# Opening of a four-block recurrent kernel: x as first transfer, fills of spare rows moved, first batch's q and k split by halves on two engines ahead of the channel mix

## The chip, the cores and the metric

The kernel runs on one core of a Trainium2 chip. The metric is the device time of one execution in microseconds, lower is better. The core's engines each run their own stream of instructions in order and wait for each other through semaphores: PE (matmul, with weight loads shown as PEld), DVE (vector), ACT (activation functions), POOL (GpSimd), and SP, which issues all the transfers of this kernel.

## The reference

A stream x of shape (4, 1024, 128) passes through four blocks. Each block normalizes x, computes an attention-like branch s and a feed-forward branch g from the normalized values, and adds s times silu(g) to x:

```python
x = L0_attn_query
xn = _layernorm(x, axis=-1)
s = _L0_attn_ref(xn, L0_attn_in_proj_w, L0_attn_out_proj_w)
g = _silu(_L0_ffn_ref(xn, L0_ffn_W_r, L0_ffn_W_k, L0_ffn_W_v, L0_ffn_mu_r, L0_ffn_mu_k))
x = x + s * g
...
```

The change touches block 0 alone. Its s is attention with 16 heads of 8 dimensions, rotary embedding of q and k, and a window of 250 positions:

```python
q, k = _apply_rope(q, k)
delta = pos[:, None] - pos[None, :]
mask = (delta >= 0) & (delta < CONTEXT)
scores = jnp.einsum('bhtd,bhsd->bhts', q, k) * D ** (-0.5)
scores = jnp.where(mask[None, None, :, :], scores, jnp.finfo(scores.dtype).min)
attn = jax.nn.softmax(scores, axis=-1)
x = jnp.einsum('bhts,bhsd->bhtd', attn, v)
```

Its g is a channel mix, which mixes each position with the one before it and passes it through three matrices:

```python
xr = mu_r * x + (1.0 - mu_r) * x_prev
xk = mu_k * x + (1.0 - mu_k) * x_prev
r = jax.nn.sigmoid(jnp.einsum('btc,dc->btd', xr, W_r))
k = jnp.einsum('btc,dc->btd', xk, W_k)
out = r * jnp.einsum('btc,dc->btd', jnp.square(jax.nn.relu(k)), W_v)
```

Block 1 has causal attention and a mixture of 8 experts, block 2 a full-attention transformer layer and a switch layer, block 3 a state-space layer and two layers of local attention.

## The kernel before

**Layout.** A batch is 1024 positions of 128 channels. Transferred to the chip it is a tile of 128 partitions by 8 by 128; after the norm (`_norm_steps`, two halves of 512 positions each, the power for the reciprocal root on POOL as `ln_rs`) PE turns it (`tr_ps`) and ACT copies it into `xT`, channels by positions.

**Projection and split.** `project(b)` in `_attention` makes q and k of one batch in halves of 512 positions: two matmuls into `proj_ps`, and three DVE operations that apply the rotation (`qd` or `kd`, and `rope_t`). To multiply with bf16 inputs at nearly fp32 precision, `_split` writes a value as three bf16 parts: a cast, a subtraction, a cast and a subtraction, lines 196 to 199. In the kernel before all four run on POOL, once for the 1024 positions of q and once for those of k. The parts are stored to DRAM (`qx`, `kx`, line 282) and read back by `load(n)` in another arrangement (lines 318 and 321): three copies into `q9` and nine into `k9` for each unit. A unit is four heads of one batch, so block 0 has 16 units; three pairs of `q9` and `k9` take turns.

**Spare rows.** `q9` and `k9` have 128 rows. Rows 0 to 71 hold the 3 by 3 products of parts. Rows 72 to 74 of `q9` later take the three parts of minus the row maximum (`negr`, line 404), which meet ones in `k9`. The remaining rows of `q9` must be zero. At the start rows 64 to 127 of all three `q9` are filled with 0.0 on DVE and those of all three `k9` with 1.0 on POOL (line 854), and 3 rows of zeros are stored to DRAM for the units from the fourth on. Two tiles `va` for the values are filled with 1.0 on POOL (line 859).

**Maxima.** `maxima(n)` multiplies q and k of a unit (`max_ps`) in 14 steps and DVE reduces each to the row maximum (`neg`). `attend(n)` does the multiplication again (`sc`), with the maximum taken off by the extra rows, then the exponential on ACT (`pt`) and the product with the values (`o_ps`).

**Channel mix.** `_channel_mix` makes half a batch in four steps: `dx` (POOL, line 658) and `xrk` (DVE), the key `kp` with a ReLU on ACT and a square on POOL (line 668), the receptance `rv` with a sigmoid, and the value.

**Order.** Matmuls, transposes and POOL's `_tt` calls keep the program's order; a scheduler places the rest on each engine by its own estimate when the program is built, so the order in the source is only part of the order that runs. `_blocks012` writes the opening: the norm of batch 0 runs, then two streams are interleaved in proportion, `begin` (projection of batch 0, loads of units 0 and 1, 14 steps of maxima of unit 0, the split of the maxima, 5 steps of maxima of unit 1) and `other` (norms of batches 1 to 3 and eight half-batch mixes), with the silu steps at the end of `other`. Then `rest` runs the units: maxima of the next unit beside the weights of this one, and on three of four units parts of the next batch's projection. All transfers are issued by SP in its own order; the first ones are w0, w1, r1, rope, and then x of batches 0 and 1.

Of the kernel before, what the change touches and what calls it, by code (L numbers as in the profile page):

```python
# [29 lines left out]
P = 128  # L30
# [157 lines left out]
def _run(steps):  # L188
    for step in steps:
        if step:  # L190
            step()
# [27 lines left out]
def _attention(k, pool, mode, xT, w, out, rope=None):  # L219
# [19 lines left out]
    def project(b):  # L239

        xb = xT[:, b, 1 : T + 1]
        steps = []
        va = dense["va", b] = k.va[b % 2]

        def half(what, hf):
            cols = slice(512 * hf, 512 * hf + 512)

            def step():
                if hf == 0:
                    dense[what] = pool.tile([P, T], F32, tag="d", name=f"{what}d", bufs=2 if mode == "window" else 1)  # L250
                d = dense[what] if hf == 0 else dense.pop(what)
                ps = ps2("proj_ps")
                matmul(ps[:, 0, :], lhsT=w[what], rhs=xb[:, cols], start=True, stop=True)
                if rope is not None:
                    matmul(ps[:, 1, :], lhsT=w[what + "s"], rhs=xb[:, cols], start=True, stop=True)
                bias = w.get("b" + what, 0.0)
                if mode == "window":

                    t2 = pool.tile([P, 512], F32, tag="rope_t", name="rope_t", bufs=2)
                    nc.vector.tensor_tensor(d[:, cols], ps[:, 0, :], rope[:, 0, cols], ALU.mult)  # L260
                    nc.vector.tensor_tensor(t2, ps[:, 1, :], rope[:, 1, cols], ALU.mult)
                    nc.vector.tensor_tensor(d[:, cols], d[:, cols], t2, ALU.add)
                else:
                    nc.scalar.activation(d[:, cols], ps[:, 0, :], AF.Identity, bias=bias)
                if rope is not None and mode != "window":
                    t2 = pool.tile([P, 512], F32, tag="rope_t", name="rope_t", bufs=2)
                    nc.scalar.activation(t2, ps[:, 1, :], AF.Identity, bias=w.get("b" + what + "s", 0.0))
                    nc.gpsimd.tensor_tensor(d[:, cols], d[:, cols], rope[:, 0, cols], ALU.mult)
                    nc.gpsimd.tensor_tensor(t2, t2, rope[:, 1, cols], ALU.mult)
                    nc.gpsimd.tensor_tensor(d[:, cols], d[:, cols], t2, ALU.add)  # L270
                if hf == 1:
                    parts = pool.tile([P, 3, T], BF16, tag="parts", name=f"{what}p", bufs=1)
                    _split(nc, nc.gpsimd, d, parts, d)
                    dense[what, "parts"] = parts

            return step

        def store(what):
            def step():

                flat = k.tc.dram_tile([3, P, T], BF16, name=f"{what}x")
                nc.sync.dma_start(flat.rearrange("s p t -> p s t"), dense.pop((what, "parts")))
                dense[what, b] = flat.rearrange("s (d h) t -> (s d) h t", h=H)

            return step

        def values(i):
            def step():
                ps = ps1("v_ps")
                for c in range(4):  # L290
                    t0 = P * (4 * i + c)
                    matmul(
                        ps[:, c * P : c * P + P], lhsT=xb[:, t0 : t0 + P], rhs=w["v"], start=True, stop=True
                    )
                vh = va[:, 4 * i : 4 * i + 4, 0 : H * (HD + 1)].rearrange("p c (h d) -> p c h d", d=HD + 1)
                of = ps.rearrange("p (c h d) -> p c h d", c=4, d=HD)
                if "bv" in w:
                    bv = w["bv"].rearrange("p (h d) -> p h d", d=HD)
                    for c in range(4):
                        nc.vector.tensor_tensor(vh[:, c, :, 0:HD], of[:, c], bv, ALU.add)  # L300
                else:
                    nc.scalar.copy(vh[:, :, :, 0:HD], of)

            return step

        for what in ("q", "k"):
            steps += [half(what, 0), half(what, 1)]

        return steps + [store("q"), lambda: None, store("k"), values(0), values(1)]
# [527 lines left out]
def _blocks012(k, t):  # L837
# [7 lines left out]
    with ExitStack() as ctx:  # L845
        pool_of = lambda name, side="left": k.tc.tile_pool(name=name, bufs=1, side=side)
        k.ps = ctx.enter_context(k.tc.tile_pool(name="ps", bufs=2, space=PSUM))
        with pool_of("w1") as wp:


            k.q9, k.k9 = ([wp.tile([P, 4, T], BF16, name=f"{n}9_{i}") for i in range(3)] for n in "qk")
            for q9, k9 in zip(k.q9, k.k9):
                nc.vector.memset(q9[64:P], 0.0)
                nc.gpsimd.memset(k9[64:P], 1.0)
            k.zeros = k.tc.dram_tile([3, 4 * T], BF16, name="zeros")
            nc.sync.dma_start(k.zeros, k.q9[2][72:75].rearrange("p h t -> p (h t)"))
            k.va = [wp.tile([P, NT, H * (HD + 1) + 32 - HD - 1], F32, name=f"va_{i}") for i in range(2)]
            for t_ in k.va:
                nc.gpsimd.memset(t_, 1.0)
            early = ctx.enter_context(ExitStack())  # L860
            wp0 = early.enter_context(pool_of("w0", "right"))
            w0 = wp0.tile([P, 9 * P + 2], F32, name="w0")
            nc.sync.dma_start(w0, t["w0"])
            names = ("q", "qs", "k", "ks", "v", "o", "wr", "wk", "wv")
            w = {n: w0[:, i * P : i * P + P] for i, n in enumerate(names)}
            mu_r, mu_k = w0[:, 9 * P : 9 * P + 1], w0[:, 9 * P + 1 : 9 * P + 2]

            w1 = wp.tile([P, 4 * P + 10], F32, name="w1")
            nc.sync.dma_start(w1, t["w1"])
            r1 = wp.tile([P, 2 * P + E8], F32, name="r1")  # L870
            nc.sync.dma_start(r1, t["r1"].to_broadcast([P, 2 * P + E8]))
            gates = {}

            def to_block1(b, gp, pool):

                g = xn[:, tiles_of(b), :]
                lg = {}

                def logits():
                    lg[0] = pool.tile([P, NT, E8], F32, name="lg", bufs=2)  # L880
                    of = lambda i: xT[:, b, 1 + i * P : 1 + i * P + P]
                    _logits(k, lg[0], of, w1[:, 4 * P + 2 : 4 * P + 10], r1[:, 2 * P : 2 * P + E8])

                def gate():
                    gates[b] = _gating(k, pool, gp, lg[0], b)

                return _update_steps(k, b, xin[b]) + _fm_steps(k, g, xT, b) + [logits, None, gate]

            with pool_of("a0") as pool:
                rope = pool.tile([P, 2, T], F32, name="rope")  # L890
                nc.sync.dma_start(rope, t["rope"][:, 0])
                wa = {n: w[n] for n in names[:6]}
                held = {}
                normed = [
                    [lambda b=b: held.update({b: _x_tile(k, xin[b])})]
                    + _norm_steps(k, lambda b=b: held[b], xn[:, tiles_of(b), :])
                    + _fm_steps(k, xn[:, tiles_of(b), :], xT, b)
                    for b in range(B)
                ]
                normed[0].insert(1, normed[1].pop(0))  # L900
                begin, rest = _attention(k, pool, "window", xT, wa, s, rope)
                _run(normed[0])
                mix = [_channel_mix(k, pool, w, mu_r, mu_k, n) for n in range(2 * B)]
                other = []
                for b in range(B):
                    other += (normed[b + 1] if b + 1 < B else []) + mix[2 * b] + mix[2 * b + 1]
                _interleave(other + _silu_steps(k, range(B)), begin)
                plan = {}
                for b in range(B - 1):
                    _put(plan, to_block1(b, wp, wp), _behind(b))  # L910
                rest(plan)
                last = to_block1(B - 1, wp, wp)
            early.close()

            with pool_of("w2", "right") as wp2:
                NW = 14 * P
                w2 = wp2.tile([P, NW + 20], F32, name="w2")
                nc.sync.dma_start(w2, t["w2"])
                r2 = wp2.tile([P, 3 * P + E8], F32, name="r2")
                nc.sync.dma_start(r2, t["r2"].to_broadcast([P, 3 * P + E8]))  # L920
                lg2 = wp2.tile([P, NTILE, E8], F32, name="lg2")
                _blocks12(k, t, wp, pool_of, gates, last, (w1, r1, w2, r2, lg2))
# [1268 lines left out]
```

## Time and profile before

| | |
|---|---|
| median of 3 runs | 3529.68 us (3518.91 to 3532.71) |
| the profiled execution | 3530.33 us, its span 3528.6 us |
| PE busy | 3137.5 us (89%) |
| DVE busy | 2458.7 us (70%) |
| ACT busy | 1985.6 us (56%) |
| POOL busy | 1415.6 us (40%) |
| mean DMA rate | 42 GB/s over the span |
| first statistics on x (DVE) | starts at 12.31 us |
| first operation of the rotation, `qd` (DVE) | starts at 24.64 us |
| store of q's parts, of k's parts issued (SP) | 37.46 us, 53.44 us |
| first `max_ps` matmul, first `sc` matmul (PE) | 67.46 us, 108.21 us |

Times in the trace count from the span's start. A row of the trace in order of time gives start, length, engine, line, operation, output and input, how many of a kind were merged, and in brackets how long the engine had been idle and what ended that. Where many rows of one kind are merged, the length is that of the whole group. DVE's calls in block 0 go through a helper and all show line 60, PE's matmuls show line 104 or 108, so the tiles' names tell them apart. Line numbers of the changed kernel are six higher behind the first edit.

### The profile page before, as it was taken

What the parts mean: (1) busy time and instruction counts of PE and PEld (TensorE: products, weight loads), DVE (VectorE), ACT (ScalarE), POOL (GpSimd) and SP (SyncE); (2) the same over time, 40 slices, a digit from 0 to 9 for tenths busy, and PEclk for the clock granted to TensorE, in tenths of its full rate; (3) what the DMA queues carried; (4) which work ended last, traced back from release to release, by engine and by line L of the source; (5) the groups of instructions that cost most, each with busy time, mean ns of one, the idle gap of its engine ahead of it and who ended that gap; (6) DMA issues with size and microseconds to landing.
All of it is one profiled execution on the core that took longest, in us unless ns stands there. A gap on an engine that the chain in (4) does not pass through costs nothing.

```text
span 3528.6 us, 63440 instructions
## 1 busy us (share of the span) xinstructions
PE 3137.5 (89%) x23982; PEld 1693.8 (48%) x24121; DVE 2458.7 (70%) x4929; ACT 1985.6 (56%) x4191; POOL 1415.6 (40%) x1969
## 2 busy tenths in 40 slices
PE   4898988999989988889998989986899989989997
PEld 3444445664434434422333323322666767766665
DVE  7667663447777865788785686844788778777675
ACT  2444453346555554455666766664665656666664
POOL 5555553003323251120340321014766656755653
PEclk8999999999999999999999999998899999999999
DMA  3322312201222211011111211102110011011010
GB/s 101 71 63 55 73 42 87 59 28 47 52 50 60 42 51 31 21 45 28 39 45 45 66 35 26 30 7 73 29 37 16 20 25 24 18 24 28 21 27 21
DMA packets 134085, 146.61 MB, mean 42 GB/s; under 512 B 80642, under 2 KB 108298, under 8 KB 126474
## 3 DMA queue, kind: packets, MB, share of 16 engines
q1 hardware_dynamic: 131732, 138.34, 16.3%
q0 software_dynamic: 2048, 4.20, 0.4%
q8 instruction: 191, 3.13, 0.4%
q14 instruction: 114, 0.93, 0.1%
HBM read 94.42 MB, written 30.11 MB: 35 GB/s over the span
## 4 chain that ended last, share of the span: by engine, by line
PE 58%; DVE 19%; ACT 9%; POOL 8%; issue 4%; DMA 2%; SPq 0%; ACTq 0%; POOLq 0%; DVEq 0%
PE o_ps L104 11%; PE max_ps L104 10%; PE sc L104 10%; DVE neg L60 6%; ACT pt L451 4%; PE op L104 4%; PE hp L104 3%; POOL rn L1573 2%; PE proj_ps L104 2%; PE lsc L1481 1%; PE lo_ps L1481 1%; PE ag_ps L1481 1%; PE qk_ps L1481 1%; PE wo_ps L1481 1%; DVE xn L60 1%
## 5 line engine op out<-in xcount | busy, mean ns | idle before, releaser
L451 ACT ACTIVATE pt<-sc 128x512 f32<-128x512 f32 (+3 forms) x2432 | 1076.2, 512 | 754.1 <-PE sc L104 698.1
L60 DVE TENSOR_REDUCE neg<-max_ps 128x1 f32<-128x1024 f32 (+6 forms) x1088 | 1171.9, 1101 | 443.6 <-PE max_ps L104 404.8
L104 PE MATMUL sc<-q,k 128*128 128x512 bf16 (+3 forms) x2399 | 643.1, 340 | 94.6 <-ACT pt L451 69.0
L104 PE MATMUL max_ps<-k,q 128*128 128x512 bf16 (+3 forms) x2200 | 611.2, 347 | 73.8 <-DVE neg L60 50.7
L104 PE MATMUL o_ps<-pt,va 128*32 128x512 f32 (+3 forms) x4864 | 562.6, 526 | 16.8 <-POOL pt L421 9.1
L421 POOL TENSOR_SCALAR_AFFINE_SELECT pt<-pt 128x256 f32<-128x256 f32 (+2 forms) x768 | 291.3, 397 | 541.7 <-ACT pt L451 537.0
L104 PEld LDWEIGHTS <-k 128*128 128x128 bf16 x2432 | 185.6, 98 | 531.5 <-issue 415.9
L104 PEld LDWEIGHTS <-q 128*128 128x128 bf16 x2304 | 217.1, 99 | 357.6 <-issue 245.6
L1643 ACT ACTIVATE pr<-lsc,nb,r 128x128 f32<-128x128 f32 x512 | 201.2, 476 | 67.9 <-DVE nb L1635 67.7
L1564 POOL TENSOR_TENSOR qn<-qn,rot 128x512 f32<-128x512 f32 x128 | 166.1, 1303 | 157.8 <-DVE rot L1556 133.2
L1573 POOL TENSOR_TENSOR rn<-ss,neghalf 128x16 f32<-128x16 f32 x64 | 188.5, 2945 | 60.5 <-DVE ss L1571 48.3
L104 PEld LDWEIGHTS o_ps<-pt,va 128*32 128x32 f32 x4864 | 100.1, 109 | 227.1 <-issue 170.8
L196 POOL CAST negp<-neg 128x32 bf16<-128x32 f32 x48 | 10.1, 211 | 477.2 <-DVE neg L60 477.1
L91 POOL TENSOR_TENSOR ln_rs<-ln_ve,neghalf 128x4 f32<-128x4 f32 x72 | 73.8, 1026 | 262.0 <-DVE ln_ve L60 246.5
L728 ACT ACTIVATE h<-hp,eb 128x512 f32<-128x512 f32 x128 | 80.8, 683 | 163.2 <-PE hp L104 157.2
L1481 PE MATMUL qk_ps<-wqkv,hT 128*128 128x512 f32 x256 | 139.2, 628 | 23.7 <-DMA wqkv<-in_w_dram 7.3
L104 PE MATMUL hp<-xT,ew 128*128 128x512 f32 x256 | 127.9, 624 | 15.5 <-DVE neg L60 12.5
L60 DVE SCALAR_TENSOR_TENSOR xn<-op,gates,xn 128x128 f32<-128x128 f32 x256 | 72.0, 344 | 99.2 <-PE op L104 99.2
L104 PEld LDWEIGHTS op<-ew,h 128*128 128x128 f32 x1024 | 124.3, 194 | 19.6 <-issue 16.3
L104 PE MATMUL max_ps<-mask_window,ident 128*128 128x268 bf16 (+1 forms) x432 | 127.0, 294 | 0.0
L104 PE MATMUL op<-ew,h 128*128 128x128 f32 x1024 | 126.2, 277 | 0.1
L104 PEld LDWEIGHTS <-ident 128*128 128x128 bf16 x864 | 85.2, 99 | 65.5 <-issue 24.6
(368 smaller groups left out, 5483.9 us busy)
## 6 DMA issues: line engine op xcount, KB each, us to landing
q<-qx SPq DMA_DIRECT2D x144, 192.0 KB
k<-kx SPq DMA_DIRECT2D x432, 64.0 KB
va<-vb SPq DMA_DIRECT2D x120, 128.0 KB
qx<-qp SPq DMA_DIRECT2D x12, 768.0 KB
kx<-kp SPq DMA_DIRECT2D x12, 768.0 KB
ew<-in_e1w_dram SPq DMA_DIRECT2D x64, 128.0 KB
x<-x SPq DMA_DIRECT2D x16, 512.0 KB
x<-in_x_dram SPq DMA_DIRECT2D x8, 512.0 KB
```

What stands on the lines that cost most here:

```text
L60: r = op(*args, **kw)
L91: nc.gpsimd.tensor_tensor(rs, ve, k.neghalf[:, :n], ALU.pow)
L104: k.tc.keep_in_program_order(k.nc.tensor.matmul(*args, **kw))
L196: eng.tensor_copy(dst[:, 0], src)
L421: nc.gpsimd.affine_select(out=pt, in_=pt, pattern=[[0, 2], [step, pt.shape[2]]], compare_op=ALU.is_ge, fill=0.0, base=base, channel_multip ...
L451: nc.scalar.activation(pt[:, j % 2, :width], sc[:, :width], AF.Exp, scale=scale)
L728: nc.scalar.activation(h[:, hh, :], hp[:, hh, :], AF.Gelu, bias=eb1[:, e, hh : hh + 1])
L1481: pin(nc.tensor.matmul(*args, **kw))
L1564: nc.gpsimd.tensor_tensor(qn[:, i], qn[:, i], rot, ALU.add)
L1573: nc.gpsimd.tensor_tensor(rn, ss.rearrange("p w h -> p (w h)"), k.neghalf[:, : 2 * NH], ALU.pow)
L1643: nc.scalar.activation(t.pr[:, h, :], t.sc[r][:, c, :], AF.Exp, bias=t.nb[r][:, c : c + 1], scale=t.r8[:, h : h + 1])
```

## The change

Four things are done, all in block 0's opening.

- x of batch 0 is the first transfer on SP. Then come w0, rope, x of batch 1, w1 and r1.
- The fills are written at other places. `va_0` is filled on DVE ahead of the first norm, `va_1` on DVE; `spare(i)` fills the spare rows of one pair: pair 0 after the first norm, pairs 1 and 2 behind the first 11 steps of `begin`, that is behind the loads of units 0 and 1. Unit 1's `q9` and `k9` are thus filled after they were loaded; rows 64 to 71, the products of the third parts of both, are overwritten there for that one unit.
- For batch 0 alone q and k are split by halves of 512 positions, as soon as a half is rotated: q on POOL, k on DVE. k has a tile of its own for the parts.
- The first 11 steps of `begin` (projection, stores, values, loads of units 0 and 1) come first, then the norm of batch 1 and the two mixes of batch 0, and only then the remaining steps are interleaved.

```diff
-                if hf == 1:
-                    parts = pool.tile([P, 3, T], BF16, tag="parts", name=f"{what}p", bufs=1)
+                first = mode == "window" and b == 0
+                if hf == 0 and first:
+                    dense[what, "parts"] = pool.tile([P, 3, T], BF16, tag=f"parts{what}", name=f"{what}p0", bufs=1)
+                if first:
+                    eng = nc.gpsimd if what == "q" else nc.vector
+                    _split(nc, eng, d[:, cols], dense[what, "parts"][:, :, cols], d[:, cols])
+                elif hf == 1:
+                    parts = pool.tile([P, 3, T], BF16, tag="partsq", name=f"{what}p", bufs=1)
                     _split(nc, nc.gpsimd, d, parts, d)
                     dense[what, "parts"] = parts
...
-            for q9, k9 in zip(k.q9, k.k9):
-                nc.vector.memset(q9[64:P], 0.0)
-                nc.gpsimd.memset(k9[64:P], 1.0)
-            k.zeros = k.tc.dram_tile([3, 4 * T], BF16, name="zeros")
-            nc.sync.dma_start(k.zeros, k.q9[2][72:75].rearrange("p h t -> p (h t)"))
             k.va = [wp.tile([P, NT, H * (HD + 1) + 32 - HD - 1], F32, name=f"va_{i}") for i in range(2)]
-            for t_ in k.va:
-                nc.gpsimd.memset(t_, 1.0)
+
+            def spare(i):
+                nc.vector.memset(k.q9[i][64:P], 0.0)
+                nc.gpsimd.memset(k.k9[i][64:P], 1.0)
+                if i == 2:
+                    k.zeros = k.tc.dram_tile([3, 4 * T], BF16, name="zeros")
+                    nc.sync.dma_start(k.zeros, k.q9[2][72:75].rearrange("p h t -> p (h t)"))
...
-            nc.sync.dma_start(w0, t["w0"])
...
-            nc.sync.dma_start(w1, t["w1"])
...
-            nc.sync.dma_start(r1, t["r1"].to_broadcast([P, 2 * P + E8]))
...
+                x0 = _x_tile(k, xin[0])
+                nc.sync.dma_start(w0, t["w0"])
                 nc.sync.dma_start(rope, t["rope"][:, 0])
+                x1 = _x_tile(k, xin[1])
+                nc.sync.dma_start(w1, t["w1"])
+                nc.sync.dma_start(r1, t["r1"].to_broadcast([P, 2 * P + E8]))
...
-                held = {}
+                held = {0: x0, 1: x1}
...
-                normed[0].insert(1, normed[1].pop(0))
+                for b in range(2):
+                    normed[b].pop(0)
                 begin, rest = _attention(k, pool, "window", xT, wa, s, rope)
+                nc.vector.memset(k.va[0], 1.0)
                 _run(normed[0])
+                spare(0)
+
+                _run(begin[:11])
+                spare(1)
+                spare(2)
+                nc.vector.memset(k.va[1], 1.0)
...
-                _interleave(other + _silu_steps(k, range(B)), begin)
+
+                beside = len(normed[1]) + 2 * len(mix[0])
+                _run(other[:beside])
+                _interleave(other[beside:] + _silu_steps(k, range(B)), begin[11:])
```

## Prediction

> **What bounds the kernel now.** I read the page first: PE is busy 89% of the span and 58% of the chain that ended last. From 160 us on its slices leave little to win. The first slice does not look like that, so I went on to the busy time by stretch, up to the first `max_ps` matmul (67.4 us) and from there to the first `sc` matmul (108.4 us).
>
> ```profile
> PE   4898988999989988889998989986899989989997
> ...
> PEclk8999999999999999999999999998899999999999
> ```
> ```profile
> 0.00:67.40 67.40, 25.73 (x88) 16.84 (x88) 48.33 (x128) 11.30 (x15) 45.59 (x44) 0.80 0.43 119
> 67.40:108.40 41.00, 33.31 (x209) 23.81 (x209) 30.24 (x36) 19.58 (x24) 10.65 (x13) 0.95 0.25 49
> ```
>
> Of the page's slices the two PE lines; in the rows by stretch the columns after the length are busy PE, PEld, DVE, ACT and POOL, then granted clock, DMA share and GB/s. PE works 25.7 of the first 67.4 us: up to 41.7 us could in principle be had. In the next 41 us PE has 33.3 busy and DVE 30.2: that stretch has room for some DVE work, not for much. After it PE sets the pace, and the order of instructions of the two programs is the same on every engine, so what the opening gains or loses is carried to the end.
>
> Then the chain in order of time and the instructions of the opening tell who is last:
>
> ```profile
> 7.76 6.96 POOL k L854 x2
> 14.77 2.39 POOL va L859 x2
> 17.15 1.01 POOL ln_rs L91
> ...
> 53.44 4.13 DMA kx<-kp
> 57.58 2.73 DMA k<-kx
> 60.33 6.89 DMA k<-kx
> 67.46 1.01 PE max_ps L104 x5
> ```
> ```profile
> 12.31 0.49 DVE L60 BATCH_NORM_STATS2 ln_st<-x 128x6 f32<-128x128 f32 x2 [2.88 <-DMA x<-in_x_dram]
> ...
> 24.64 0.68 DVE L60 TENSOR_TENSOR qd<-proj_ps,rope 128x512 f32<-128x512 f32 x1
> ...
> 35.39 4.03 DVE L60 SCALAR_TENSOR_TENSOR xrk<-dx,w,xT 128x512 f32<-128x512 f32 x2 [1.92 <-POOL dx L658]
> ...
> 46.77 3.43 DVE L60 TENSOR_SCALAR xn<-x,ln_mv,ln_rs 128x128 f32<-128x128 f32 x3
> ...
> 51.29 2.12 POOL L199 TENSOR_TENSOR kp<-kd,kp 128x1024 bf16<-128x1024 f32 x1
> ...
> 138.98 0.48 PE L104 MATMUL sc<-q,k 128*128 128x384 bf16 x2 [2.42 <-DMA q<-negr]
> ```
>
> POOL's fills hold the first norm (`ln_rs`) to 17.15. Then q's split, k's split and the channel mix stand in one row on POOL: k is whole at 53.4, and k's way through DRAM (`kx`, then the `k9` copies) takes 67.46 - 53.44 = 14.0 us. So the opening is one path: x, norm, projection, splits, DRAM, first maxima.
>
> **The change, part by part.** I walk that path in the order of instructions that the changed program was built with. It differs from the old one only in the opening.
>
> *x first.* Before, x lands at 12.31, behind w0, w1, r1 and rope. The copy of batch 2, alone, was issued at 20.35 and had moved its bytes by 23.5. A first copy issued at 0.79 therefore lands near 4.5 (4.0 to 5.5).
>
> *First norm to first rotation.* The gain of 8 us does not last. The first half's statistics take 1.6 us (12.31 to 13.9), `ln_rs` 1.0. But then POOL's order is: fill of `k9_0` 3.51, a mask select 0.50, fill of `k9_2` 3.51, and only then `ln_rs` of the second half. That is 4.5 + 1.6 + 1.0 + 7.5 + 1.0 = 15.6. PE's order has all eight transposes ahead of the first projection, so half a norm is of no use. On DVE the fill of `va_1` (1336 of 2048 columns of the 1.76 us fill of q: 1.15), batch 1's statistics and its `xn` also stand before the first `qd`, with two more `ln_rs` in turn. Without any waiting for POOL's fills the first `qd` comes at 4.5 + 16 = 20.5; with them (before, the CAST of `ident16` took 2.00 us beside a fill, until its end) at 4.5 + 18.6 = 23.1. I take 22.5, against 24.64.
>
> *Splits.* DVE issues for q and k 12 rope operations at 0.61 apart, and now k's split besides: 8 operations, of which 4 are subtractions of 512 columns (0.68) and 4 casts. No row shows such a cast on DVE: its ends are half a 512-column operation (0.3) and all of it (0.68); I take 0.3, as its neighbour `xn` (128 columns from SBUF, 0.27) is nearest. Ahead of k's last part stand three `xn` (0.3) and one `xrk` (0.75): 7.3 + 2.7 + 1.2 + 0.9 + 0.75 = 12.9, and some waits for the projection's PSUM make it 13.5. Beside it POOL splits q: half of 1.03 + 2.12 + 1.03 + 2.12 per half, 6.3 in all, and two `dx` of 1.03. In the fence above two `xrk` took 4.03 beside POOL's `qp` and `dx`, where one alone takes 0.74, and three `xn` took 3.43: DVE and POOL take turns. Ordered so, one by one, I get 17.8 for k's end, with the full price of POOL's row; some of it falls beside PSUM reads, which did not wait (`kd` from PSUM took 0.68 beside POOL's subtraction). I take 17 (13.5 to 19). So `kx` is issued at 22.5 + 17 = 39.5, not 53.44 (ends 34 to 43.5). q is ready earlier: 11.2 after the first `qd`, and its store lands 3.6 later (37.46 to 41.06), before 39.5.
>
> The Trainium skill speaks against splitting on two engines at once (SBUF — State Buffer, section Who interferes with whom): a DVE operation with two SBUF inputs, or a cast in a two-port mode, and a GpSimd operation that reads SBUF exclude each other for a whole instruction. The 4.03 us agree. By that rule alone k ends 17.8 after the first `qd` and the time is 0.8 above mine; if the engines did not meet, 3.5 below it.
>
> *Through DRAM.* Before, the third copy of q's rows had gone out at 53.88, ahead of k's copies. Now it stands between the sixth and the ninth `k9` copy. From 60 to 70 us the copies moved at 88 GB/s, so 192 KB cost 2.1 us; if they overlap, nothing. First maxima: 39.5 + 14.0 + 2.1 = 55.6, against 67.46: 11.9 earlier. Both mixes of batch 0 lie between: their `xrk` follow k's split, and by the old durations (kp 1.9, rv 1.9, kr 1.0, rv 1.1, twice, and one `ln_rs`) they end about 10.5 us after `kx`, 5 us before PE needs the maxima. That cover costs nothing, and if k's copies were over 5 us faster, the mixes would be late next.
>
> *What was hidden and is no longer.* Before, all four norms were done by 60.5. Now batch 3's norm (8 statistics, 8 `xn`, two `ve`: 5.4 us at the spacing of 12.31 to 15.3 and 22.34 to 23.19) and `q9_1`'s fill (1.76) stand on DVE between the tenth and the eleventh of 14 maxima, and on POOL `k9_1`'s fill (3.51) ahead of batch 3's `ln_rs`. Both fills wait for unit 1's copies, as these write some of the same rows. Before, unit 1's last copy went out at 71.9; 3 us later it has landed, 7.5 after the first maxima, and DVE and POOL reach the fills some 11 to 16 after them. So they don't wait, they only take their time: 7.2 us on DVE in a stretch of 41 with 10.8 idle. Transposes of batch 3 wait for them, and the mixes of batches 2 and 3 behind these on PE. Bounds 0 (it fills idle time) and 8.5 (all, and an `ln_rs`); I take 4.5, the middle, since neither end has a row nearer to it.
>
> *Queue order later.* At 138.98 PE waited 2.42 us for `negr` of unit 1, whose copy was issued behind `qx` and two loads of x (1 MB). These loads now stand ahead of `qx`. Gain 2.4 (0 to 2.4).
>
> *At no cost:* w1 and r1 land later, under work that needs neither before the gates; values of batch 0 go before the mixes, while PE idles; the store of zeros is first read by the fourth load; `va_0`'s fill lies before x lands.
>
> **Sum.** -11.9 + 4.5 - 2.4 = -9.8. The profiled execution took 3530.33 us (span 3528.6 and 1.7 around it), 0.65 above the median 3529.68 of runs between 3518.91 and 3532.71. Predicted: 3530.3 - 9.8 = 3520.5.
>
> **Rivals.**
> - *The engines hardly meet* and the norm of batch 3 fills idle time: first `qd` at 20.5, `kx` at 34.0, maxima at 48.0, 19.5 earlier, and 2.4 from the queue: 3508.4. For it: fills of q and k lay side by side unslowed (1.76 and 3.51), and DVE has idle time where the norm goes. Against: 4.03 and 3.43.
> - *Given back:* what is won before the maxima is lost after them, since the moved norm and fills delay in-order PE by their 8.5 and the splits take 19: maxima 8 earlier, sum about 0: 3530. For it: DVE 30.2 + 7.2 of 41 in a stretch where each mix goes through four engines.
> - *Slower: `k9_1`'s fill holds POOL.* It stands ahead of batch 3's `ln_rs` and four mixes' `dx` and `kr`. At half the old rate of copies unit 1 would land 17.5 us later, 25 after the first maxima, 14.5 after POOL is there: with the fill's own 3.5 that is 18 more, 3538. It decides once the landing is some 13 us later than I have it, and is worse than 0.5% from 30 on. Against: the copies depend on nothing but `kx`.
> - That x comes first is worth little by itself is already in the sum (2 us at the first `qd`).
>
> **Numbers.** My forecast 0.50 (its own range 3512 to 3530), hardly meeting 0.26, given back 0.16, slower 0.08. 0.5% is 17.6 us, about what a measurement of this kernel can tell from no change: 3512.0 to 3547.3. Faster: the second case, and a little of the first: 0.28. Slower by over 0.5%: most of the last, 0.06. Within: 0.66. The range takes the second case and the third with the runs' scatter of some 3 to 5 us: 3505 to 3535.
>
> **What would show it.** In the profile after: statistics on x near 4.5; first `qd` 20 to 24; `kx` issued 34 to 44; first `max_ps` 48 to 60; q's and k's casts alternating in time; batch 3's norm after the tenth `neg`; first `sc` near 101, not 108.2; no wait for `negr` near 130. I am wrong if POOL's `k9_1` fill starts long after the square of mix 3, if PE has something else than k's copies to wait for before the maxima, or if later stages move by more than the opening.

## The result, and the profile after

The changed kernel takes 3521.89 us in the median of 12 runs (3510.54 to 3531.09), beside 3531.61 us for the kernel before on the same chip: a ratio of 0.9975 with a 95% interval of 0.9964 to 0.9985. That is 8.8 us less (5.3 to 12.7), within 0.5%. The profiled execution took 3521.42 us, its span 3519.7.

The forecast was 3520.5 us. The marks of the opening, in us from the span's start, show how this came about:

| mark | before | forecast | after |
|---|---|---|---|
| first statistics on x | 12.31 | 4.5 | 4.59 |
| first `qd` | 24.64 | 22.5 | 21.24 |
| store of k's parts issued (`kx`) | 53.44 | 39.5 | 38.26 |
| first `max_ps` | 67.46 | 55.6 | 54.53 |
| first `sc` | 108.21 | about 101 | 106.37 |
| the `sc` that needs `negr` of unit 1 | 138.98 | no wait | 135.16 |

Up to the first maxima the change gains 12.9 us, where 11.9 had been forecast. From there to the first `sc` it loses 11.1 of them, where 4.5 had been expected. In the profiles at hand another 3.5 us come back at `negr` of unit 1, where 2.4 had been expected.

First PE's slices on the page of the changed kernel, then its rows by stretch (length, busy PE, PEld, DVE, ACT and POOL, then granted clock, DMA share, GB/s), up to the first `max_ps`, the first `sc`:

```profile
PE   5898988999989988889998989987889999999897
```
```profile
0.00:54.50 54.50, 24.61 (x84) 15.02 (x84) 44.26 (x111) 10.72 (x14) 31.63 (x38) 0.82 0.48 138
54.50:106.40 51.90, 37.37 (x212) 26.08 (x213) 35.66 (x63) 20.29 (x25) 17.80 (x17) 0.86 0.41 71
```

The first slice of PE has gone from 4 to 5 tenths; of the other 39, five differ by one tenth, three up and two down. The first stretch is 12.9 us shorter. The second is 51.9 us long, where the kernel before had 41.0: DVE has 63 instructions there instead of 36, since a whole norm has moved in, and PE is at a clock of 0.86 instead of 0.95.

The chain of waits of this execution goes back to 102.9 us only, so instructions in order of time stand in for it (start, length, engine, line, operation; in brackets the idle time before it and what ended it). DVE and then POOL in the first 40 us (the fills of `k9` show line 862 here):

```profile
4.59 0.49 DVE L60 BATCH_NORM_STATS2 ln_st<-x 128x6 f32<-128x128 f32 x2
...
9.58 5.50 DVE L60 TENSOR_SCALAR xn<-x,ln_mv,ln_rs 128x128 f32<-128x128 f32 x3
...
21.24 0.69 DVE L60 TENSOR_TENSOR qd<-proj_ps,rope 128x512 f32<-128x512 f32 x1 [0.24 <-PE proj_ps L104]
...
31.19 1.64 DVE L60 TENSOR_TENSOR kd<-kd,rope_t 128x512 f32<-128x512 f32 x1
32.75 2.42 DVE L60 CAST kp<-kd 128x512 bf16<-128x512 f32 x2
...
36.55 0.42 DVE L60 CAST kp<-kd 128x512 bf16<-128x512 f32 x1
```
```profile
7.34 3.51 POOL L862 MEMSET k<- 64x4096 bf16 x1
...
11.49 3.51 POOL L862 MEMSET k<- 64x4096 bf16 x1
15.09 1.02 POOL L91 TENSOR_TENSOR ln_rs<-ln_ve,neghalf 128x4 f32<-128x4 f32 x1
...
30.61 1.66 POOL L199 TENSOR_TENSOR qp<-qd,qp 128x512 bf16<-128x512 f32 x1
32.24 2.65 POOL L664 TENSOR_TENSOR dx<-xT 128x512 f32<-128x512 f32 x2
```

x is there 7.7 us earlier, but the second `ln_rs` starts at 15.09, behind two fills. While k and q are split, DVE and POOL stretch each other: the last operation of k's rotation (`kd<-kd,rope_t`) takes 1.64 us beside POOL's `qp`, where the same operation on q took 0.69, and a cast that takes 0.42 us alone takes 1.2 beside the two `dx`. Then the stage of the maxima, on PE and on DVE:

```profile
54.53 0.58 PE L104 MATMUL max_ps<-k,q 128*128 128x128 bf16 x4 [3.75 <-DMA k<-kx]
...
78.31 1.38 PE L108 MATMUL tr_ps<-ident,xn 128*128 128x128 f32 x4 [6.46 <-DVE xn L60]
...
106.37 0.49 PE L104 MATMUL sc<-q,k 128*128 128x384 bf16 x2
...
135.16 0.48 PE L104 MATMUL sc<-q,k 128*128 128x384 bf16 x2 [0.40 <-DMA q<-negr]
135.49 1.88 PE L104 MATMUL proj_ps<-xT,w 128*128 128x512 f32 x4
```
```profile
73.33 1.76 DVE L60 MEMSET q<- 64x2048 uint32 x1 [0.48 <-issue]
75.13 0.49 DVE L60 BATCH_NORM_STATS2 ln_st<-x 128x6 f32<-128x128 f32 x2
...
79.81 1.84 DVE L60 TENSOR_SCALAR xn<-x,ln_mv,ln_rs 128x128 f32<-128x128 f32 x4 [0.65 <-POOL ln_rs L91]
81.57 0.94 DVE L60 TENSOR_REDUCE neg<-max_ps 128x2 f32<-128x768 f32 x1
```

PE stands 6.46 us at 71.85, until the first transposes of batch 3, and these wait for DVE, which from 73.33 to 81.57 does the fill of `q9_1` and the norm of batch 3, and no reduction.

### The profile page after: what moved, and what is told of

It is laid out like the page before. It is cut to its first block, busy times and chain, and to the rows that moved or that the text cites. A ratio compares the mean times of both kernels' runs of the same rounds, so it can differ in the third digit from the quotient of the medians.

```text
span 3519.7 us, 63444 instructions
## 1 busy us (share of the span) xinstructions
PE 3130.8 (89%) x23982; PEld 1689.5 (48%) x24121; DVE 2460.4 (70%) x4939; ACT 1987.5 (56%) x4191; POOL 1410.6 (40%) x1967
## 3 DMA queue, kind: packets, MB, share of 16 engines
q8 instruction: 191, 3.13, 0.4%
## 4 chain that ended last, share of the span: by engine, by line
PE 57%; DVE 18%; ACT 9%; POOL 7%; issue 4%; DMA 2%; SPq 0%; ACTq 0%; POOLq 0%; DVEq 0%
PE o_ps L104 11%; PE max_ps L104 10%; PE sc L104 10%; DVE neg L60 6%; ACT pt L457 5%; PE op L104 4%; PE hp L104 3%; POOL rn L1594 2%; PE proj_ps L104 2%; PE lsc L1502 1%; PE lo_ps L1502 1%; PE ag_ps L1502 1%; PE qk_ps L1502 1%; PE wo_ps L1502 1%; PE qkt_ps L1505 1%
## 5 line engine op out<-in xcount | busy, mean ns | idle before, releaser
L104 PEld LDWEIGHTS op<-ew,h 128*128 128x128 f32 x1024 | 123.4, 192 | 19.6 <-issue 16.3
```

Source lines behind the costliest of these rows:

```text
L104: k.tc.keep_in_program_order(k.nc.tensor.matmul(*args, **kw))
```

## The experiments

Each run's times are compared with those of the kernel before on its own chip. Marks in us:

| run | first `qd` | `kx` | first `max_ps` | first `sc` | from one to the other | ratio to before (95%) |
|---|---|---|---|---|---|---|
| before | 24.64 | 53.44 | 67.46 | 108.21 | 40.8 | |
| before, again | 24.66 | 53.46 | 68.24 | 111.06 | 42.8 | 0.9994 (0.9981 to 1.0007) |
| changed | 21.24 | 38.26 | 54.53 | 106.37 | 51.8 | 0.9975 (0.9964 to 0.9985) |
| changed, again | 21.26 | 38.27 | 54.60 | 106.35 | 51.8 | 0.9969 (0.9958 to 0.9980) |
| pair 1 filled early | 24.9 | 42.24 | 59.00 | 110.35 | 51.4 | 0.9969 (0.9953 to 0.9986) |
| norms early | 21.0 | 37.97 | 76.39 | 115.02 | 38.6 | 0.9996 (0.9982 to 1.0010) |
| both | 24.9 | 42.24 | 78.45 | 119.3 | 40.9 | 1.0007 (0.9995 to 1.0019) |
| both splits on POOL | 21.5 | 43.58 | 60.38 | 109.5 | 49.2 | 0.9983 (0.9969 to 0.9997) |
| x3 and norms early | 20.90 | 37.84 | 54.07 | 97.66 | 43.6 | 0.9965 (0.9952 to 0.9979) |
| old transfer order | 25.50 | 42.51 | 59.14 | 110.66 | 51.5 | 0.9984 (0.9974 to 0.9993) |
| old interleave | 25.07 | 44.58 | 58.92 | 101.49 | 42.6 | 0.9964 (0.9950 to 0.9978) |
| x3, norms, next loads early | 20.91 | 37.86 | 54.41 | 97.94 | 43.5 | 0.9958 (0.9943 to 0.9972) |
| the same, fills on ACT | 17.59 | 34.63 | 51.44 | 96.89 | 45.5 | 0.9947 (0.9931 to 0.9962) |

**Which of the late pieces gives the gain back?** In the runs that fill pair 1 behind unit 1's load, rows 64 to 71 are overwritten for that unit as in the changed kernel; the others keep them. Three theories stood: (A) the norm of batch 3 between the maxima, (B) the fills of pair 1, (C) neither, but the way of each mix through four engines. The first run moves the fill alone:

```diff
                 spare(0)
+                spare(1)
                 _run(begin[:11])
-                spare(1)
                 spare(2)
```

> Edit: the fills of pair 1 (q9_1 on DVE 1.76 us, k9_1 on POOL 3.51) move from the stage of the maxima into the first 15 us, behind those of pair 0; nothing else moves. In the changed kernel first max_ps is at 54.53 and first sc at 106.37, 51.8 apart, where the kernel before has 67.46 and 108.21, 40.8 apart: 11.1 us are given back. Theory A: the hole of 73.3 to 81.6 us (PE 3.11 busy of 8.30) is DVE standing with the fill and then the norm of batch 3; the fill is its first 1.8 us, and k9_1's 3.51 on POOL is covered by it. Then the first qd comes up to 3.5 later (POOL's row ahead of the second ln_rs is one fill longer), first max_ps near 57.5, max_ps to sc 49 to 50, and the time stays within 2 us of the changed kernel's. Theory B: the fills alone make the loss (k9_1 holds the chain of the mixes on POOL): max_ps to sc falls to 42 to 45, first sc near 100, 5 us faster. Theory C: neither, the mixes' way through four engines sets the pace: max_ps to sc stays 51 to 52 and the time is 3 us worse.

From the first `max_ps` to the first `sc` it takes 51.4 us, instead of 51.8. B falls as far as this order goes. PE's wait for norm 3 shrinks by the fill (4.01 us instead of 6.46), but what this saves is spent further on: the mix behind it runs at half clock (its two `kp` matmuls take 1.91 us instead of 1.02), and PE waits 2.12 us for a `kr` that it waited 1.03 for. So A's 49 to 50 was missed as well. The first `qd` is 3.7 us later: one more fill on POOL ahead of the norm costs its whole length.

Then the norms of batches 2 and 3 ahead of the maxima, without and with that fill:

```diff
-                other = []
-                for b in range(B):
-                    other += (normed[b + 1] if b + 1 < B else []) + mix[2 * b] + mix[2 * b + 1]
-                beside = len(normed[1]) + 2 * len(mix[0])
+                other = normed[1] + mix[0] + mix[1] + normed[2] + normed[3]
+                beside = len(other)
+                for b in range(1, B):
+                    other += mix[2 * b] + mix[2 * b + 1]
```

> Edit: the norms of batches 2 and 3 and their transposes stand ahead of the first maxima on DVE and PE, as in the kernel before; the mixes of batches 1 to 3 stay between the maxima; the fills of pair 1 stay where they are in the program, which now puts q9_1's ahead of the first reduction on DVE. Theory A (norm of batch 3 in the stage of the maxima makes the loss): max_ps to sc falls from 51.8 to 41 to 45. But two norms (10 us of DVE) stand where there were 3.75 us of slack, and q9_1's fill waits for the copies of unit 1: first max_ps moves from 54.5 to 59 to 63. First sc 101 to 106, time 0 to 5 us better than the changed kernel. Theory C (the way of the mixes sets the pace): max_ps to sc stays near 50, first sc 109 to 112, time 3 to 6 worse.

> Both edits: the fills of pair 1 in the first 15 us, and the norms of batches 2 and 3 ahead of the first maxima. Theory A: max_ps to sc as in the kernel before, 40 to 43; first max_ps near 60 (3 later for the fill on POOL, 3 for the norms); first sc 100 to 103, that is 3 to 6 us better than the changed kernel, time near 3517. Theory C: max_ps to sc near 50 and first sc near 110, time near 3525.

The stage of the maxima shrinks to 38.6 and 40.9 us, as A says: without norm 3 in it, it is as short as in the kernel before. But the first maxima come 22 and 24 us later, far beyond what was expected, and the kernels end at the time of the kernel before. On DVE of the run with norms alone the reason stands in two rows:

```profile
64.28 1.76 DVE L60 MEMSET q<- 64x2048 uint32 x1 [12.54 <-DMA q<-qx]
70.22 0.49 DVE L60 BATCH_NORM_STATS2 ln_st<-x 128x6 f32<-128x128 f32 x2 [4.18 <-DMA x<-in_x_dram]
```

The fill waits for unit 1's copies, and norm 3 for its x: the load is issued at 59.97, in SP's queue behind unit 1's copies, and lands 10 us later. With the fill out of the way DVE waits 17.47 us for this one load, until 72.25. So x of batch 3 bounds norm 3 from below; to move the norm, the load has to be moved too.

**The load and the norms together.** The four batches take two buffers for x in turn, so x of batch 3 gets a tile of its own:

```diff
+                x3 = pool.tile([P, NT, C], F32, tag="x3", name="x3", bufs=1)
+                nc.sync.dma_start(x3, xin[3])
+                x2 = _x_tile(k, xin[2])
...
+                other = normed[1] + mix[0] + mix[1] + normed[2][:4] + normed[3][:4]
+                beside = len(other)
+                other += normed[2][4:] + mix[2] + mix[3] + normed[3][4:]
+                for b in range(2, B):
+                    other += mix[2 * b] + mix[2 * b + 1]
```

> Edit: x of batch 3 gets a tile of its own and is loaded right behind the first transfers instead of behind unit 1's copies; the norms of batches 2 and 3 (without their transposes) are issued ahead of the maxima, the fills of pair 1 fall behind the maxima by the resulting order. In the two runs with norms early, max_ps to sc was 38.6 and 40.8 us, against 51.8 in the changed kernel, but the first max_ps came at 76.4 and 78.4, since norm 3 waited for x (landed 70.2, issued at 60 behind unit 1's copies) and DVE for q9_1's fill. Theory A (norm of batch 3 between the maxima is what gives the gain back): now first max_ps 55 to 58 and max_ps to sc 39 to 43, so first sc 96 to 99 against 106.37; 5 to 8 us faster than the changed kernel, about 3515. Its loads of x for the next block stand behind qx again, so PE's wait for negr of unit 1 may return (about 2.4, and 1.5 for a slow projection behind it). Theory C (the mixes' way through four engines sets the pace, and a longer max_ps is the price of any early norm): first sc stays at 104 to 108.

Its row for the stage of the maxima, and then PE in order of time:

```profile
54.07:97.66 43.59, 34.62 (x208) 24.19 (x208) 32.00 (x43) 19.46 (x24) 16.13 (x16) 0.93 0.26 49
```
```profile
54.07 0.59 PE L104 MATMUL max_ps<-k,q 128*128 128x128 bf16 x4 [3.69 <-DMA k<-kx]
...
87.73 0.58 PE L104 MATMUL max_ps<-k,q 128*128 128x128 bf16 x4 [1.93 <-POOL k L862]
...
128.59 0.79 PE L104 MATMUL sc<-q,k 128*128 128x384 bf16 x2 [2.58 <-DMA q<-negr]
129.17 3.31 PE L104 MATMUL proj_ps<-xT,w 128*128 128x512 f32 x4
```

A holds: the first maxima stay where they were, and the stage takes 43.59 us. Norm 3 (with the fill of `q9_1`, which moves behind it) was worth 51.84 - 43.59 = 8.2 us, and the first `sc` comes 8.7 earlier. The 8.2 is a net figure: in this order PE waits 1.93 us for `k9_1`'s fill, which it did not in the changed kernel, and a wait of 2.11 us for `kr` that the changed kernel has at 92.04 is gone. The loads of x for the next block fall behind `qx` again, and PE waits 2.58 us for `negr` of unit 1, with a slow projection behind it: 4.5 to 4.9 of the 8.7 us are left at 155 us, against the two profiles of the changed kernel. The ratio of 0.9965 can't be told from the changed kernel's.

**The next block's loads.** One more edit writes these two loads ahead of batch 1's projection:

```diff
                 for b in range(B - 1):
-                    _put(plan, to_block1(b, wp, wp), _behind(b))
+                    steps = to_block1(b, wp, wp)
+                    if b < 2:
+                        steps[0]()
+                        steps[0] = None
+                    _put(plan, steps, _behind(b))
```

> The kernel with x of batch 3 and the norms early (first sc 97.66, then a wait of 2.58 us for negr of unit 1 and a projection of 3.31 instead of 1.9 us), with one edit: the two loads of x for the next block are issued behind negr of unit 0, ahead of qx. Theory: these two loads (1 MB) ahead of negr are what PE waits for: wait 0 to 0.5, projection 1.9, and the maxima behind it 8 to 9 ahead of the changed kernel instead of 4.5. Time 6 to 9 us below the changed kernel at 160 us, as far as the clock lets it stand. Rival: the wait is the DMA's own latency behind negr and stays 2.5.

SP's queue and PE of this run:

```profile
84.68 1.89 SPq L410 DMA_DIRECT2D q<-negr  x3
86.61 1.22 SPq L166 DMA_DIRECT2D x<-in_x_dram  x2
...
118.88 0.38 SPq L288 DMA_DIRECT2D qx<-qp  x1
121.70 1.77 SPq L410 DMA_DIRECT2D q<-negr  x3
```
```profile
126.38 0.49 PE L104 MATMUL sc<-q,k 128*128 128x384 bf16 x2
126.70 1.88 PE L104 MATMUL proj_ps<-xT,w 128*128 128x512 f32 x4
```

The loads now stand between `negr` of unit 0 and `qx`, the wait is gone, the projection takes 1.88 us, and the maxima at 155 us in the changed kernel are 8.8 us earlier. The rival (the DMA's own latency) falls.

**The second engine.** k's split goes back to POOL, the order stays:

```diff
-                    eng = nc.gpsimd if what == "q" else nc.vector
+                    eng = nc.gpsimd
```

> Edit: k's split back on POOL, still by halves and ahead of the channel mix. Theory: DVE and POOL take turns, so two engines save little: q's and k's splits are 12.6 us of POOL, and k would end some 22 us after the first qd if POOL is never opposed (first qd, one half's wait, then 12.6 and two dx), against 17.0 measured with two engines. kx issue near 43 to 44 instead of 38.26, first max_ps 59 to 60, first sc 106 to 110: most of the gain ahead of the maxima comes from splits standing ahead of the mix, 4 to 6 of 15 us from the second engine. Rival: the split on two engines is the whole gain: kx near 50. The loads of x also stand behind qx again here as in the kernel before: by the explanation of the queue PE waits about 2.4 us for negr of unit 1, and the projection behind that wait takes 3.4 instead of 1.9 us; by the rival (the wait vanished since the whole stage had more slack) there is no such wait.

As expected, `kx` is issued at 43.58: the second engine is worth 5.3 us of the 15.2. What splitting by halves is worth by itself, no run separates. On POOL alone a cast of a half takes 0.6 us and a subtraction 1.15 to 1.6. The loads of x stand behind `qx`, and the wait (2.49 us) and the slow projection (3.40) are back. This run also shows the price of a fill that A leaves out: norm 3 stands ahead of the maxima here (DVE has 37 instructions in the stage, the changed kernel 63), and still it takes 49.2 us to the first `sc`, since `k9_1`'s fill now stands late on POOL, and the maxima of unit 1 wait for it:

```profile
98.65 0.58 PE L104 MATMUL max_ps<-k,q 128*128 128x128 bf16 x4 [4.51 <-POOL k L862]
```

**x first.** The transfers go back to their old order:

```diff
-                x0 = _x_tile(k, xin[0])
                 nc.sync.dma_start(w0, t["w0"])
-                nc.sync.dma_start(rope, t["rope"][:, 0])
-                x1 = _x_tile(k, xin[1])
                 nc.sync.dma_start(w1, t["w1"])
                 nc.sync.dma_start(r1, t["r1"].to_broadcast([P, 2 * P + E8]))
+                nc.sync.dma_start(rope, t["rope"][:, 0])
+                x0 = _x_tile(k, xin[0])
+                x1 = _x_tile(k, xin[1])
```

> Edit: w0, w1, r1 and rope are transferred ahead of x again, all else as in the changed kernel. Theory: x lands near 12.3 as in the kernel before; as POOL's two fills are then over before the second ln_rs is wanted, the first qd comes at 23.5 to 24.7 (changed kernel 21.24, before 24.64), so x first is worth 2.3 to 3.5 us; kx issue 40.6 to 41.7, first max_ps 57 to 58, first sc 108.5 to 110. Rival: x first is worth the full 7.7 us by which the first statistics moved, first qd at 29; or nothing, first qd at 21 to 22.

The first `qd` comes at 25.50, 4.3 us later than in the changed kernel, and every mark up to the first `sc` is late by as much. That is more than the 2.3 to 3.5 expected. On POOL only one of the two fills is over before x is there; the second keeps its place behind the first `ln_rs`, and the second `ln_rs` comes behind it at 19.05:

```profile
14.19 1.03 POOL L91 TENSOR_TENSOR ln_rs<-ln_ve,neghalf 128x4 f32<-128x4 f32 x1 [6.49 <-DVE ln_ve L60]
15.28 3.51 POOL L862 MEMSET k<- 64x4096 bf16 x1
19.05 1.01 POOL L91 TENSOR_TENSOR ln_rs<-ln_ve,neghalf 128x4 f32<-128x4 f32 x1 [0.26 <-DVE xn L60]
```

**The written order.** Is it needed to write the splits ahead of the mix?

```diff
                 spare(0)
-
-                _run(begin[:11])
                 spare(1)
                 spare(2)
...
-                beside = len(normed[1]) + 2 * len(mix[0])
-                _run(other[:beside])
-                _interleave(other[beside:] + _silu_steps(k, range(B)), begin[11:])
+                _interleave(other + _silu_steps(k, range(B)), begin)
```

> Edit: the opening's order in the program is again one interleave of channel mix and attention, as in the kernel before, with all three pairs filled ahead of it; x first and k's split by halves on DVE stay. The resulting order still puts the splits ahead of the mix on DVE, and loads x of batches 2 and 3 ahead of qx. Theory: the written front-loading (first eleven steps at once) is not what gains, and is what pushes norm 3 between the maxima. First qd 24.9 (one more fill on POOL, as in the run with that fill early), kx issue 42 to 44, first max_ps 58 to 61 with norm 3 ahead of it, max_ps to sc 40 to 43, first sc 99 to 103, so 3 to 7 us ahead of the changed kernel there; the loads of the next block's x stand behind qx, so PE waits about 2.5 for negr of unit 1 and 1.5 more. Rival: without the front-loading the splits fall back behind the mix, kx near 50 and first sc near 108.

It is not. `kx` is issued at 44.58, not near 50: with halves on two engines the scheduler puts the splits ahead of the mix by itself, and x of batches 2 and 3 is loaded ahead of `qx`. Of its delay against the changed kernel (6.3 us) 3.8 is the third fill on POOL ahead of the first `qd`; the other 2.5 were not taken apart. The stage of the maxima takes 42.6 us, and the first `sc` is 4.9 us ahead of the changed kernel's. PE then waits 2.72 us, here put down to a copy of k, and has a projection of 3.13 us, so that 1.1 us are left; the ratio can't be told from the changed kernel's.

**The fills away from POOL.** On top of the kernel with x3, the norms and the next loads early, ACT fills two of three `k9`, and all fills are written ahead of the projections:

```diff
-                nc.gpsimd.memset(k.k9[i][64:P], 1.0)
+                if i == 0:
+                    nc.gpsimd.memset(k.k9[i][64:P], 1.0)
+                else:
+                    nc.scalar.activation(k.k9[i][64:P], k.q9[i][64:P], AF.Exp)
...
                 spare(0)
+                spare(1)
+                spare(2)
                 _run(begin[:11])
-                spare(1)
-                spare(2)
```

> As the run before it, and the spare rows of k9_1 and k9_2 are filled by ACT (exp of q's zeros) in the first 15 us, all three pairs ahead of the projections. POOL then has one fill ahead of the second ln_rs. Theory: POOL's fills set the first qd: 3.5 less gives 17 to 18 instead of 20.9, kx issue 33 to 35, first max_ps 49.5 to 51.5. But norm 1 now stands behind the splits on DVE with norms 2 and 3 (16 us between k's split and the first reduction), so the first reduction comes at 54 to 57 and first sc at 94 to 98. Rival: x's landing and DVE bind the first qd, which stays within 1 us of 20.9.

POOL of this run has the second `ln_rs` at 11.45 instead of 15.09, and the first `qd` follows:

```profile
7.38 3.51 POOL L863 MEMSET k<- 64x4096 bf16 x1
...
11.45 1.01 POOL L91 TENSOR_TENSOR ln_rs<-ln_ve,neghalf 128x4 f32<-128x4 f32 x1
```
```profile
17.59 0.69 DVE L60 TENSOR_TENSOR qd<-proj_ps,rope 128x512 f32<-128x512 f32 x1 [0.22 <-PE proj_ps L104]
```

POOL's fills had set the first `qd`. Of the 3.3 us that it gains, 3.0 are left at the first maxima and 1.1 at the first `sc`, since three norms now stand between k's split and the first reduction, which starts at 59.0, later than the 54 to 57 expected. At 145 us it is 10.1 us ahead of the changed kernel. Its median is 3510.86 us, a ratio of 0.9947 (0.9931 to 0.9962) to the kernel before: the fastest of all, 5.3 thousandths below it where the changed kernel is 2.5 and 3.1 below. The two kernels were not run on the same chip, and the interval touches the changed kernel's second one.

**How far a single profile carries.** The changed kernel and the kernel before were profiled once more:

> The changed kernel, unedited, for a second profiled execution. The marks of the opening should agree with the first within 0.3 us (first qd 21.2, kx 38.3, first max_ps 54.5, first sc 106.4); later stages, above all from 2310 us on, may differ by some us, as far as the granted clock of the two profiles differs. If the opening's marks differ by more than 1 us, single profiles can't carry the readings.

> The kernel before, unedited, for a second profiled execution. In the two profiles of the changed kernel the opening is 5.3 and 5.8 us ahead at 160 us, but the spans are 8.9 and 12.6 us shorter, and the difference grows only behind 2310 us, where nothing was changed. If that growth is the clock of single executions, this profile agrees with the first one to 0.5 us up to 160 us and parts from it by some 3 to 6 us behind 2310; its span may lie anywhere from 3522 to 3532. If the later gain belongs to the change, this profile agrees with the first one to 1 us up to the end. The ratio of its times to those of the kernel before should hold 1 in its interval.

The marks of the changed kernel repeat to 0.1 us. Those of the kernel before repeat only as far as `kx`: its second profile has the first `sc` at 111.06, 2.9 us later, with a clock of 0.90 instead of 0.95 between the maxima and the `sc`. About half of this shows at one place: both executions wait 1.76 us for the same `kr`, but behind that wait the first goes on at full clock (`rv` 1.13 us at 99.52) and the second at half (`rv` 2.04 us at 100.91). So my expectation of 0.5 us was wrong, and the 11.1 us that were given back are 9.0 against this second profile. The spans of these two executions of one kernel are 3528.6 and 3517.3 us: the second is 2.9 us behind at 160 us, 1.3 ahead at 2734 and 10.9 ahead at 3447. A difference of spans between two profiles says nothing here; the ratios of many runs do, and 0.9994 (0.9981 to 1.0007) for the unedited kernel shows what these are good for.

## Why the prediction was right, and where it was not

- **x first, first norm to first rotation.** Taken 22.5 for the first `qd` (20 to 24.5), measured 21.24. POOL's order was as said, `ln_rs`, fill, select, fill, `ln_rs`, with the second ending at 16.1 (15.6 worked out). DVE's `xn` did stand still beside the second fill (three of them 5.50 us), but this ran beside POOL's fill, which was waited for anyway. So the value nearer to "no waiting" was right. The run with the old transfer order puts x first at 4.3 us at the first `qd`, about twice the 2 us of the prediction's last rival.
- **Splits.** Taken 17 us from the first `qd` to the end of k (13.5 to 19), measured 38.26 - 21.24 = 17.0. That it agrees to a tenth is chance, as the range was 5.5 us wide. The engines took turns as in the old rows: `kd` 1.64 us beside `qp` 1.66, two casts 2.42 beside two `dx` 2.65. The cast that no row had shown takes 0.42 us unopposed, and the next operation starts 0.34 behind its start, where 0.3 was taken. The Trainium skill (SBUF — State Buffer, section Who interferes with whom) has DVE operations with two SBUF inputs and casts in a two-port mode exclude POOL's reads for a whole instruction. These rows agree, while `kd` from PSUM took 0.68 us in the same stretch.
- **Through DRAM.** Taken 14.0 + 2.1, measured 54.53 - 38.26 = 16.3. (192 KB at 88 GB/s are 2.2 us, not 2.1.) The mixes of batch 0 were over 3.75 us before the maxima, where 5 had been expected: they cost nothing, and DMA was the last to arrive.
- **What was hidden and is no longer.** This is the step that failed. I took 4.5 us as the middle of 0 and 8.5, since neither end had a row nearer to it. The run that takes norm 3 out of the stage without delaying the maxima measures 8.2 us net, near the upper end. DVE's idle time in the stage was no cover, as it did not lie where the norm stands: DVE did the fill and the norm in one piece of 8.2 us (73.33 to 81.57), PE's order has the transposes of batch 3 in front of the next maxima, and so both stood. The stage lost 9.0 to 11.1 us in all. Part of what goes beyond the norm is PE at half clock behind the hole: the four transposes at 78.31 take 1.38 us, at a granted clock of 0.50 from 78.3 to 82.3, where eight take 1.27 at 58.13. Another part stands at 92.04: there PE waits 2.11 us for `kr`, as POOL now has the split of the maxima (`negp`, from 89.36) ahead of that square (90.95), and `kp` and `rv` behind the wait take 2.02 and 1.50 us instead of 1.02 and 1.05; in the kernel before the square (92.85) stood ahead of `negp` (95.37), and PE waited 0.44 us. What each of these is worth was not measured by itself.
- **The fills.** That they would not wait was right in the changed kernel (`k9_1`'s starts at 67.92, behind the square of mix 3) and is a matter of their place: put earlier, `q9_1`'s fill waited 12.54 us for unit 1's copies; put later, maxima waited 4.51 us for `k9_1`'s. The rival in which they hold an engine is real, but did not come about here.
- **Queue order later.** Taken 2.4, at the upper end of 0 to 2.4; measured 3.5: 2.0 of the wait (2.42 to 0.40) and 1.5 of the projection behind it (3.41 to 1.88 us). The mechanism was right and is shown by the run that moves only the loads. What was missing was the clock: the wait that went took a slow projection with it.
- **The sum.** -9.8 was forecast. -12.9 + 11.1 - 3.5 is -5.3 at the maxima of 160 us against the first profile of before; the second one, 2.9 us later there, makes it -8.2. The ratios give -8.8 (-12.7 to -5.3) and for the second set -10.9 (-14.8 to -7.0). The forecast lies in both, and that it comes so near is in part luck: its errors have opposite signs, +1.0 to +1.8 at the maxima (54.53 against the two profiles of before), -4.5 to -6.6 behind them, +1.1 at the queue. What lies between the 5.3 to 8.2 us at 160 us and the 8.8 to 10.9 us of the medians was not taken apart.
- **The rivals.** "Given back" described the stage better than the forecast: 9.0 to 11.1 of the 12.9 to 13.7 us were lost again by the first `sc`; the queue kept it from being the whole story. The engines did meet. `k9_1`'s fill did not hold POOL beyond its own 3.51 us.

## What to carry to other kernels

Work that is moved off the path to the first result does not vanish: ask where the engine's order puts it next, and whether the idle time that is to hide it lies at that place and in one piece. A late load can tie a whole norm to the end of a queue of copies, so look at what stands ahead of it in that queue before moving what it feeds. Compare an edit by the marks of its own stage in two profiles of each kernel, not by one difference of spans.

## What the runs showed of the hardware

- A short wait of PE can be followed by half clock, and its length alone does not decide. Five waits of 2.42 to 2.72 us were each followed by a projection of 3.08 to 3.41 us, and without them the same four matmuls took 1.88. Of five waits of 2.11 us for `kr`, four were followed by half clock; the one with pair 1 filled early was not. The same wait of 1.76 us in the two profiles of the kernel before was followed by full clock in one and by half in the other. In the openings of these profiles a stretch at half clock lasts 3.41 us or a multiple of it: 139.51 to 142.92 in the kernel before, 100.53 to 103.95 in its second profile, both at a granted clock of 0.50. In the 3.41 us ahead of them PE was busy for 0.99 and 1.42 us. In the first profile the 1.76 us lie across two such stretches, in which PE was busy for 2.02 (95.14 to 98.55) and 2.45 us (98.55 to 101.97), and the clock stayed at 1.00. The Trainium skill (TensorE: Matmul & The Clock Gate, Part 1) gives one idle window of about 3.4 us as the condition; here the shorter waits were enough, and the measurement decides.
- ACT fills 64 by 4096 bf16 through the exponential of zeros in 3.61 us, POOL's fill of the same size takes 3.51.
- Three `xn` of 128 columns took 5.50 us beside a fill on POOL that reads nothing; in the run with fills on ACT, where the second fill is gone, they took 2.19.
